# Mamba block: output weights centred once, variance of the output tiles summed on ScalarE

## The chip, the cores and the metric

The kernel runs on one core of a Trainium2 chip. The metric is the device time of one execution in microseconds (us). One core has five engines that run side by side, each with its own instruction queue worked off in order: TensorE (PE; its weight loads are listed apart as PEld), VectorE (DVE), ScalarE (ACT), GpSimd (POOL) and SyncE (SP, which here only issues DMAs).

## The reference, cut to what matters

The program is a network of several layers on an image of 2 x 256 channels x 32 x 32. The first layer after a group normalisation is a pair of Mamba blocks, and only this layer is touched. The sequence is the image itself, 1024 tokens of 256 channels, two of them in the batch.

```python
def layernorm(x, w, b):
    mu = jnp.mean(x, axis=-1, keepdims=True)
    var = jnp.mean(jnp.square(x - mu), axis=-1, keepdims=True)
    return (x - mu) * jax.lax.rsqrt(var + LN_EPS) * w + b

def mamba_block(x, ...):
    xs, res = jnp.split(u @ in_w + in_b, 2, axis=-1)   # 512 channels each
    xs = silu(conv(xs) + conv_b)                       # depthwise, 4 taps
    dt, Bm, Cm = jnp.split(xs @ xproj_w, ...)          # 16 states
    delta = softplus(dt @ dt_w + dt_b)
    dA = jnp.exp(delta * A);  dBu = delta * Bm * xs
    h = dA_t * h + dBu_t                               # scan over the 1024 tokens
    y = sum over states of h * C_t;  y = y + xs * Dp
    y = y * silu(res)
    out = y @ out_w + out_b                            # 512 -> 256 channels
    return out
...
x = x + layernorm(mamba_block(x, ...), ln1_w, ln1_b)   # likewise with m2, ln2
```

The layernorm runs over the 256 channels of `out`. Since `out` is linear in `out_w` and `out_b`, its mean over the channels is zero once each row of `out_w` (256 numbers) and `out_b` have had their own mean taken off.

## The kernel before, in words

**Units.** `layer0` (L766) cuts the 2 x 1024 tokens of each block into four chunks of 512 (`TC`), so that there are eight units, 0 to 3 for block m1 and 4 to 7 for m2. A chunk has four row tiles of 128 tokens (`TPC`), and the 512 inner channels are four chunks of 128 partitions (`NDC`).

**Steps of a unit.** `enter` (L381) makes the input projection (TensorE) and adds its bias on ScalarE (`m_pre`, L405). `front` (L408) makes the depthwise convolution as products with diagonal matrices on TensorE (L430), the projections to B, C and dt, and then `delta` and `du`: `powers` is a chain of ScalarE operations (L502, L504, L509, L511), `sums` four operations for each half, which in all units but the first GpSimd does. `scan` (L546) goes through the 16 states. For each, SyncE fetches the row of B (`m_b`), GpSimd makes h = du*b in two halves of 1024 columns, ScalarE makes exp(delta*A) into PSUM, 512 columns at a time (`m_da`, L617, three buffers), VectorE scans (L621), TensorE transposes h into PSUM tiles of tokens by channels (`m_ht`, L575 or L577, three buffers), and each tile is multiplied with C and summed: on VectorE into `m_ya` (L591), or, for the states 1, 4, 7, 10 and 13, on ScalarE into a tile of its own (`m_s`, L589), which a DMA issued by GpSimd's queue adds to `m_yb` three states later. "12_3" is the fourth channel chunk of state 12.

**The step around the change.** `back` (L641) closes a unit. It makes the gate (L655), adds up y on TensorE and multiplies with the gate on VectorE (L680 to L689), and makes the output product for the four row tiles: a row of ones times the bias row (L696) and four products with `out_sb` (L700). Two row tiles share one PSUM tile of 512 columns; the pool of these tiles has two buffers, which all the projections of all the steps share. The layernorm is `norm_rows` (L181) with ScalarE as the engine of the last step: for each row tile `bn_stats` (L188) and `bn_aggr` (L189) on VectorE, a subtraction to negate the means (L192), the logarithm and the exponential on ScalarE that give 1/sqrt(var + eps) (`rstd`, L159 and L160), a multiplication on VectorE (L200), and four scalings with scale and bias on ScalarE (L202). The normalised rows are transposed back (L213), ScalarE applies `ln_w` and `ln_b` (L724), and GpSimd adds the residual (L737). In the last unit VectorE does this with the residual in one (L717).

**What sets the order.** The scan of unit u is the frame. `paced` (L743) deals out steps of other generators to its 63 slots, one slot after each scan of 512 columns: the `front` of unit u+1, the `enter` of unit u+2, and the `back` of unit u-1, whose products and norm fall in slots 45 to 58, that is, states 11 to 14. The numbers in a part are how many steps, first slot, last slot. Each engine works its instructions off in the order that the framework's scheduler gives them; operations on GpSimd go through `net.lined` (L174, recorded as L179), which fixes their order to that of the program text. The weights of the output product come in through `load_rest` (L361, out_w at L369): for m1 before the first unit, for m2 in unit 4. The last `back` has no scan beside it: `both` (L898) mixes it with the convolution of the next layer on TensorE.

Of the kernel before, what the change touches and what calls it, by code (L numbers as in the profile page):

```python
# [10 lines left out]
F32 = mybir.dt.float32  # L11
I32 = mybir.dt.int32
BF16 = mybir.dt.bfloat16
AF = mybir.ActivationFunctionType
# [5 lines left out]
P = 128  # L20
# [4 lines left out]
C = 256  # L25
# [4 lines left out]
TPC = TC // P  # L30
DI = 512
NDC = DI // P
# [37 lines left out]
class Net:  # L70
# [83 lines left out]
        at -= self.rows_from  # L154
        return self.rows[:, at : at + w]

    def rstd(self, out, var):

        self.nc.scalar.activation(out, var, AF.Ln, bias=self.eps5)  # L159
        self.rooted = self.nc.scalar.activation(out, out, AF.Exp, scale=-0.5)  # L160

    def functions(self, which, *after):
# [18 lines left out]
    def norm_rows(self, outs, ins, by=None):  # L181


        nc, n = self.nc, len(ins)
        mv = self.small.tile([P, n, 2], F32, tag="ln_mv", name="ln_mv")
        for i, a in enumerate(ins):
            st = self.small.tile([P, 6], F32, tag="ln_st", name="ln_st")
            nc.vector.bn_stats(out=st, in_=a)  # L188
            nc.vector.bn_aggr(out=mv[:, i, :], in_=st)  # L189
        if by is nc.scalar:  # L190
            off = self.small.tile([P, n], F32, tag="ln_off", name="ln_off")
            nc.vector.tensor_sub(off, self.zeros[:, :n], mv[:, :, 0])  # L192
        rs = self.small.tile([P, n], F32, tag="ln_rs", name="ln_rs")
        if by is nc.gpsimd:
            nc.gpsimd.tensor_scalar_add(rs, mv[:, :, 1], self.eps5)
            nc.gpsimd.tensor_tensor(rs, rs, self.power[:, :n], ALU.pow)
        else:
            self.rstd(rs, mv[:, :, 1])
        if by is nc.scalar:
            nc.vector.tensor_mul(off, off, rs)  # L200
            for i, (o, a) in enumerate(zip(outs, ins)):
                nc.scalar.activation(  # L202
                    o, a, AF.Identity, scale=rs[:, i : i + 1], bias=off[:, i : i + 1]
                )
            return
        for i, (o, a) in enumerate(zip(outs, ins)):
            nc.vector.tensor_scalar(o, a, mv[:, i, 0:1], rs[:, i : i + 1], ALU.subtract, ALU.mult)

# [78 lines left out]
class Mamba:  # L287
# [73 lines left out]
    def load_rest(self):  # L361

        net, nc, m, wpool = self.net, self.net.nc, self.m, self.wpool
        in_w, out_w, xproj_w, dt_w = self.weights
        self.gate_sb = wpool.tile([P, NCC, DI], F32, tag="gate_w", name=f"{m}_gate_sb")
        nc.sync.dma_start(self.gate_sb, in_w[:, :, DI:])
        yield
        self.out_sb = wpool.tile([P, NDC, C], F32, tag="out_w", name=f"{m}_out_sb")
        nc.sync.dma_start(self.out_sb, out_w)  # L369

        if self.kept:
            nc.sync.dma_start(self.skip_tile(), self.kept[1])
        else:
            self.scaled(self.skip_tile(), f"{m}_D")
        yield

    @staticmethod
    def first(j):
# [262 lines left out]
    def back(self, j, last=False, joined=True):  # L641


        net, nc, m, xt = self.net, self.net.nc, self.m, self.xt
        y, *sums = self.chunks.pop(j)
        tok = slice(j * TC, (j + 1) * TC)
        gate = self.one.tile([P, NDC, TC], F32, tag="gate", name=f"{m}_gate_{j}")
        for dc in range(NDC):
            ps = self.ps_mm.tile([P, TC], F32, tag="mm", name=f"{m}_g_{j}_{dc}")
            for kc in range(NCC):  # L650
                nc.tensor.matmul(
                    ps, lhsT=self.gate_sb[:, kc, dc * P : (dc + 1) * P], rhs=xt[:, kc, tok],
                    start=(kc == 0), stop=(kc == NCC - 1),
                )
            nc.scalar.activation(  # L655
                gate[:, dc, :], ps, AF.Identity, bias=net.col(f"{m}_in_b", NDC + dc)
            )
            if joined and dc == NDC - 1:
                net.gates.append(gate)
            yield  # L660
        if not joined:
            with net.tc.issue_after(net.decayed.ins):
                silu = nc.scalar.activation(gate, gate, AF.Silu)
            net.functions(EXP_LN, silu)
            yield
        if last:
            tail = self.tail(f"{m}_tail_{j}")
            for cc in range(NCC):
                x = tail[:, (2 + cc) * TC : (3 + cc) * TC]
                at = j % (HW // TC) * TC  # L670
                nc.sync.dma_start(x, self.x[j // (HW // TC), cc, :, at : at + TC])
                net.lined(nc.gpsimd.tensor_scalar_add, x, x, net.col(f"{m}_ln_b", cc))
                net.lined(nc.gpsimd.tensor_add, xt[:, cc, tok], xt[:, cc, tok], x)
                yield

        if not last:
            sums = sums[:1]
        for dc in range(NDC):
            ps = self.ps_mm.tile([P, TC], F32, tag="mm", name=f"{m}_y_{j}_{dc}")
            nc.tensor.matmul(  # L680
                ps, lhsT=self.skip[:, dc, :], rhs=y[:, dc, :], start=True, stop=False
            )
            for k, ya in enumerate(sums):
                for i in range(TPC):
                    nc.tensor.matmul(
                        ps[:, i * P : (i + 1) * P], lhsT=ya[:, i, dc * P : (dc + 1) * P],
                        rhs=net.ident, start=False, stop=(k == len(sums) - 1 and i == TPC - 1),
                    )
            nc.vector.tensor_mul(y[:, dc, :], ps, gate[:, dc, :])  # L689
            yield  # L690
        found = []
        for i in range(TPC):
            if i % 2 == 0:
                ps = self.ps_mm.tile([P, TC], F32, tag="mm", name=f"{m}_out_{j}_{i}")
            a = ps[:, i % 2 * C : (i % 2 + 1) * C]
            nc.tensor.matmul(  # L696
                a, lhsT=net.ones_row, rhs=self.out_b, start=True, stop=False
            )
            for dc in range(NDC):
                nc.tensor.matmul(  # L700
                    a, lhsT=y[:, dc, i * P : (i + 1) * P], rhs=self.out_sb[:, dc, :],
                    start=False, stop=(dc == NDC - 1),
                )
                if dc == 1:
                    yield
            found.append(a)
            yield
        if not last:
            tail = y.rearrange("p d t -> p (d t)")
        inputs = []  # L710
        tiles = [tail[:, i * C : (i + 1) * C] for i in range(TPC)]
        net.norm_rows(tiles, found, nc.scalar)
        yield
        for cc in range(NCC):
            ps = net.transposed(self.ps_mm, tiles, cc, "mm")
            if last:
                nc.vector.scalar_tensor_tensor(  # L717
                    xt[:, cc, tok], ps, net.col(f"{m}_ln_w", cc), xt[:, cc, tok],
                    ALU.mult, ALU.add,
                )  # L720
                yield
                continue
            r = tail[:, (2 + cc) * TC : (3 + cc) * TC]
            nc.scalar.activation(  # L724
                r, ps, AF.Identity, scale=net.col(f"{m}_ln_w", cc), bias=net.col(f"{m}_ln_b", cc)
            )
            if self.x is not None:
                x = self.one.tile([P, TC], F32, tag="x", name=f"{m}_x_{j}_{cc}", bufs=2)
                at = j % (HW // TC) * TC
                nc.sync.dma_start(x, self.x[j // (HW // TC), cc, :, at : at + TC])  # L730
                inputs.append(x)
            yield
        if last:
            return
        for cc in range(NCC):
            r = tail[:, (2 + cc) * TC : (3 + cc) * TC]
            net.lined(nc.gpsimd.tensor_add, xt[:, cc, tok], xt[:, cc, tok], r)  # L737
            if self.x is not None:
                net.lined(nc.gpsimd.tensor_add, xt[:, cc, tok], xt[:, cc, tok], inputs[cc])
            yield  # L740
# [25 lines left out]
def layer0(net, x, x_dram, m1, m2, load_image, taps, conv_dram, lg):  # L766
# [4 lines left out]
    tc, nc = net.tc, net.nc  # L771
    with (
# [45 lines left out]
        for u, (m, j) in enumerate(units):  # L818
# [4 lines left out]
            steps = [(b, NDC, 4, 20) for b in done]  # L823
# [19 lines left out]
                steps.append((blocks[1].fetch_diagonals(), 1, 34, 35))  # L843
            rest = m.load_rest() if u and j == 0 else iter(())
            steps += [(rest, 1, 37, 38)]
            for n, first, end in Mamba.STEPS:
                steps += [(f, n, first, end) for f in fronts]
            steps += [(b, 8, 45, 53) for b in done]
# [1459 lines left out]
```

## Time and profile before

| | |
|---|---|
| median of three runs | 2036.39 us (2035.79 to 2037.86) |
| the profiled execution's own time | 2038.11 us |
| its span in the trace | 2036.4 us |
| granted TensorE clock, mean | 0.968 |
| TensorE busy | 1864.1 us (92%), 9938 products |
| VectorE busy | 1333.6 us (65%), 2141 instructions |
| GpSimd busy | 1070.5 us (53%), 726 |
| ScalarE busy | 946.7 us (46%), 1713 |

By stage, busy us in stretches of about one unit (the last two rows are the end of the Mamba layer and all the rest):

| stretch | length | PE | DVE | ACT | POOL |
|---|---|---|---|---|---|
| 15 to 120 (opening, unit 0) | 105 | 89.76 | 83.20 | 71.76 | 80.73 |
| 120 to 237 (unit 1) | 117 | 97.80 | 107.78 | 89.53 | 98.49 |
| 237 to 354 (unit 2) | 117 | 102.88 | 107.10 | 91.71 | 100.29 |
| 354 to 472 (unit 3) | 118 | 105.84 | 107.97 | 90.83 | 100.63 |
| 1000 to 1042 (last `back`) | 42 | 41.12 | 18.14 | 4.52 | 9.66 |
| 1042 to 2036 (other layers) | 994 | 939.05 | 440.99 | 222.11 | 239.37 |

How to read the lines of the profile further down. A row of a group names line, engine, operation, result<-operands with partitions x elements, and the count; after the first bar the busy time in us and the mean of one in ns; after the second the engine's idle time just before these instructions and what ended most of it ("<-POOL m_h L179": the wait for GpSimd's m_h ended last). A row of a timeline begins with the start in us and the duration; brackets show the idle time just before and what ended it. In a window's row stand the stretch, its length and, for each engine, the busy us and the number of instructions. A row of DMA issues ends with KB each and us from issue to landing.

### The profile page before, as it was taken

The page shows a single profiled execution, that of the slowest core. Times are in us where ns is not written, and L with a number is a line of the kernel's source. Part 1 is how long each engine was busy: PE and PEld are TensorE (multiplying, and loading weights), DVE is VectorE, ACT ScalarE, POOL GpSimd, SP SyncE. Part 2 cuts the span into 40 slices and gives each one's busy share as a digit, 9 for nine tenths or more (in the row PEclk, how much of TensorE's full clock was granted, in tenths as well). Part 3 has the DMA queues.
Part 4 walks back from the last instruction along what each step waited for, and adds up shares of the span by engine and source line. Part 5 has one row for each costly group of instructions (what it writes and reads, how often), then busy time and mean ns, then how long its engine had stood idle before and what let it go on. Part 6 is the DMA issues. An engine that isn't in the chain of part 4 may idle for free. (4 is left out here: it accounts for less than half of the span.)

```text
span 2036.4 us, 27880 instructions
## 1 busy us (share of the span) xinstructions
PE 1864.1 (92%) x9938; PEld 1339.2 (66%) x9938; DVE 1333.6 (65%) x2141; ACT 946.7 (46%) x1713; POOL 1070.5 (53%) x726
## 2 busy tenths in 40 slices
PE   8788988988898988899999999999999899999995
PEld 3464665656565665655656555668999666799994
DVE  6988998998889989898515285774222345652223
ACT  4777777777887767764302253332111123221111
POOL 7888796978979698985405250012333100033330
PEclk8989999999999999899999999999999999999997
DMA  4334354343435334361130100147999300359995
GB/s 151 98 91 118 86 126 133 83 118 82 131 98 140 81 86 112 87 158 47 31 57 1 52 1 1 42 179 265 322 334 343 140 21 21 143 206 319 328 329 182
DMA packets 98856, 271.77 MB, mean 133 GB/s; under 512 B 35915, under 2 KB 54224, under 8 KB 82324
## 3 DMA queue, kind: packets, MB, share of 16 engines
q1 hardware_dynamic: 81268, 198.03, 29.0%
q0 software_dynamic: 14432, 68.31, 13.5%
q10 hardware_dynamic: 3008, 3.55, 0.5%
q8 instruction: 83, 1.36, 0.3%
q14 instruction: 65, 0.53, 0.1%
HBM read 200.80 MB, written 22.77 MB: 110 GB/s over the span
## 5 line engine op out<-in xcount | busy, mean ns | idle before, releaser
L179 POOL TENSOR_TENSOR m_h<-m_du,m_b 128x1024 f32<-128x1024 f32 x254 | 604.5, 2473 | 140.7 <-PE m_ht L577 59.0
L617 ACT ACTIVATE m_da<-m_delta,m_aneg 128x512 f32<-128x512 f32 x512 | 349.4, 694 | 149.6 <-DVE m_h L621 144.5
L621 DVE TENSOR_TENSOR_SCAN m_h<-m_da,m_state,m_h 128x512 f32<-128x512 f32 x256 | 313.9, 1266 | 22.5 <-POOL m_h L179 14.7
L577 PEld LDWEIGHTS m_ht<-ident,m_h 128*128 128x128 f32 x1600 | 194.0, 146 | 193.5 <-issue 65.6
L621 DVE TENSOR_TENSOR_SCAN m_h<-m_da,m_h 128x512 f32<-128x512 f32 x256 | 298.9, 1204 | 19.3 <-ACT m_da L617 13.4
L577 PE MATMUL m_ht<-ident,m_h 128*128 128x128 f32 x1600 | 255.1, 287 | 60.2 <-DVE m_h L621 28.8
L591 DVE SCALAR_TENSOR_TENSOR m_ya<-m_ht,m_ct,m_ya 128x512 f32<-128x512 f32 x324 | 231.3, 732 | 54.8 <-PE m_ht L577 49.8
L2067 PEld LDWEIGHTS h<-xts,we_l_late 128*128 128x128 f32 x2048 | 239.6, 193 | 9.0 <-issue 4.2
L2067 PE MATMUL h<-xts,we_l_late 128*128 128x128 f32 x2048 | 241.0, 276 | 4.5 <-SPq L2129 1.7
L2075 DVE TENSOR_TENSOR hid<-hid,h 128x512 f32<-128x512 f32 x79 | 54.2, 686 | 235.1 <-PE h L2067 234.7
L1806 POOL DMA_INDIRECT x_l_early<-l_zs,l_source x15 | 17.3, 1154 | 341.1 <-ACT pt L1570 138.9
L2074 ACT ACTIVATE hid<-h 128x512 f32<-128x512 f32 x79 | 47.1, 597 | 315.0 <-PE h L2067 315.0
L575 PE MATMUL m_ht<-ident,m_h 128*128 128x128 f32 x896 | 136.8, 300 | 30.1 <-ACT m_s L589 13.2
L575 PEld LDWEIGHTS m_ht<-ident,m_h 128*128 128x128 f32 x896 | 120.5, 206 | 53.2 <-DVE m_h L621 17.1
L1806 POOL DMA_INDIRECT x_l_late<-l_zd,source x64 | 65.4, 1022 | 148.0 <-PE xt L2050 143.9
L2082 PE MATMUL o<-we_l_late,hid 128*128 128x256 f32 x512 | 122.7, 381 | 4.1 <-DVE y L2087 2.8
L2089 POOL DMA_INDIRECT l_yd<-y,target x64 | 65.4, 1022 | 106.8 <-DVE y L2087 94.5
L589 ACT ACTIVATE m_s<-m_ht,m_ct 128x512 f32<-128x512 f32 x156 | 104.4, 686 | 29.8 <-DMA m_yb<-m_s 14.8
L430 PE MATMUL m_conv<-m_pre,m_taps 128*128 128x512 f32 x240 | 115.8, 600 | 2.5 <-ACT m_xs L436 2.5
L2082 PEld LDWEIGHTS o<-we_l_late,hid 128*128 128x128 f32 x512 | 91.8, 190 | 15.3 <-DVE y L2087 3.9
L1001 PE MATMUL early_acc<-x,early 128*98 128x448 f32 (+24 forms) x308 | 98.6, 446 | 0.4 <-DVE lg L1018 0.4
L1001 PE MATMUL acc<-x,pair 128*98 128x416 f32 (+21 forms) x308 | 93.4, 451 | 0.0
(412 smaller groups left out, 3117.4 us busy)
## 6 DMA issues: line engine op xcount, KB each, us to landing
we_l_late<-in_l_experts_dram SPq DMA_DIRECT2D x64, 1536.0 KB, 9.1
m_yb<-m_s POOLq DMA_DIRECT2D x39, 1024.0 KB, 8.6
m_b<-m_bd SPq DMA_DIRECT2D x128, 256.0 KB, 3.5
we_l_early<-in_l_experts_dram SPq DMA_DIRECT2D x15, 1536.0 KB, 8.9
m_ya<-m_yb POOLq DMA_DIRECT2D x7, 1024.0 KB, 8.9
w<-in_l_w_dram SPq DMA_DIRECT2D x21, 256.0 KB, 6.2
l_yl<-l_yd SPq DMA_DIRECT2D x8, 512.0 KB, 11.9
l_zd<-l_z SPq DMA_DIRECT2D x7, 512.0 KB, 3.2
```

The lines of the kernel that those rows point to most:

```text
L179: self.line = do(*args, **named)
L430: nc.tensor.matmul(ps, lhsT=self.taps[:, dc * 4 + k, :], rhs=pre[:, dc, k : k + TC], start=(k == 0), stop=(k == 3),)
L575: nc.tensor.matmul(a, lhsT=h, rhs=net.ident, start=True, stop=True)
L577: nc.tensor.transpose(a, h, net.ident)
L589: nc.scalar.activation(to[:, i, :], ps, AF.Copy, scale=c)
L591: nc.vector.scalar_tensor_tensor(ya[:, i, :], ps, c, ya[:, i, :], ALU.mult, ALU.add)
L617: net.decayed = nc.scalar.activation(da, delta[:, dc, :], AF.Exp, scale=self.aneg[:, i : i + 1])
L621: nc.vector.tensor_tensor_scan(h, da, h, 0.0 if first else state[:, n, dc : dc + 1], ALU.mult, ALU.add)
L1001: nc.tensor.matmul(a[:, lo - 16 * k : hi - 16 * k, co : co + n], lhsT=lhsT, rhs=self.x[:, kc, b, lo - r0 : hi - r0, ci : ci + n], start=(u ...
L1806: nc.gpsimd.indirect_dma_start(out=x, out_offset=None, in_=rows[:, :], in_offset=bass.IndirectOffsetOnAxis(ap=source[:, g : g + 1], axis=0 ...
L2067: nc.tensor.matmul(ps[:, at], lhsT=w12[:, s, kc, at], rhs=xt[:, kc * P : (kc + 1) * P], start=(kc == 0), stop=(kc == NCC - 1),)
L2082: gate.o = nc.tensor.matmul(ps[:, :C], lhsT=ht[:, mc * P : (mc + 1) * P], rhs=w[:, 8 + mc, :], start=(mc == 0), stop=(mc == NHC - 1),)
```

## The change

Each block gets a step `centre`, run on ScalarE once: for each of the four chunks of `out_w` and for the bias row, a copy in place that also sums each row (`accum_out`), two scalings of the sums by -1/256, and five additions in place of these negative means. It is a part of ten steps with the slots 6 to 36 of the block's second unit (units 1 and 5), that is, ahead of the block's first output product in slot 45 of the same unit. With centred weights the output tiles have no mean, and `back` norms them without `norm_rows`: after the product of each row tile ScalarE squares the tile and sums the squares (the squares themselves go to a tile that nobody reads), `rstd` takes the sums with a scale of 1/256, and four ScalarE copies scale the tiles. `bn_stats`, `bn_aggr`, the negation and the multiplication on VectorE go, eight times each (the first two 32 times). `norm_rows` loses its ScalarE branch; its other callers are as before. SyncE's queue and the order of GpSimd's instructions are the same in both programs. The scheduler, which is free to move ScalarE's instructions, puts the centring of m1 and both bias rows at the head of ScalarE's queue, ahead of the first `m_pre`, and that of m2 into unit 5 at states 0 to 5.

```diff
-    def rstd(self, out, var):
+    def rstd(self, out, var, scale=1.0):
-        self.nc.scalar.activation(out, var, AF.Ln, bias=self.eps5)
+        self.nc.scalar.activation(out, var, AF.Ln, bias=self.eps5, scale=scale)
         self.rooted = self.nc.scalar.activation(out, out, AF.Exp, scale=-0.5)
...
             nc.vector.bn_stats(out=st, in_=a)
             nc.vector.bn_aggr(out=mv[:, i, :], in_=st)
-        if by is nc.scalar:
-            off = self.small.tile([P, n], F32, tag="ln_off", name="ln_off")
-            nc.vector.tensor_sub(off, self.zeros[:, :n], mv[:, :, 0])
         rs = self.small.tile([P, n], F32, tag="ln_rs", name="ln_rs")
...
-        if by is nc.scalar:
-            nc.vector.tensor_mul(off, off, rs)
-            for i, (o, a) in enumerate(zip(outs, ins)):
-                nc.scalar.activation(
-                    o, a, AF.Identity, scale=rs[:, i : i + 1], bias=off[:, i : i + 1]
-                )
-            return
...
+    def centre(self):
+        nc, w = self.net.nc, self.out_sb
+        sums = self.wpool.tile([P, NDC + 1], F32, tag="centre", name=f"{self.m}_centre", bufs=1)
+        parts = [(w[:, dc, :], sums[:, dc : dc + 1]) for dc in range(NDC)]
+        parts.append((self.out_b, sums[:1, NDC:]))
+        for a, s in parts:
+            nc.scalar.activation(a, a, AF.Copy, accum_out=s)
+            yield
+        nc.scalar.activation(sums[:, :NDC], sums[:, :NDC], AF.Copy, scale=-1.0 / C)
+        nc.scalar.activation(sums[:1, NDC:], sums[:1, NDC:], AF.Copy, scale=-1.0 / C)
+        for a, s in parts:
+            nc.scalar.activation(a, a, AF.Identity, bias=s)
+            yield
...
-        found = []
+        found, squares = [], net.small.tile([P, TPC], F32, tag="ln_sq", name="ln_sq")
+        square = self.one.tile([P, C], F32, tag="square", name=f"{m}_square_{j}")
         for i in range(TPC):
...
+            nc.scalar.activation(square, a, AF.Square, accum_out=squares[:, i : i + 1])
             found.append(a)
             yield
...
-        net.norm_rows(tiles, found, nc.scalar)
+        rs = net.small.tile([P, TPC], F32, tag="ln_rs", name="ln_rs")
+        net.rstd(rs, squares, 1.0 / C)
+        for i, (o, a) in enumerate(zip(tiles, found)):
+            nc.scalar.activation(o, a, AF.Copy, scale=rs[:, i : i + 1])
         yield
...
+            if j == 1:
+                steps.append((m.centre(), 10, 6, 36))
```

The second half of a PSUM tile (row tiles 1 and 3) now has a product that waits for ScalarE's square of the first half, by the dependence that the framework keeps for each tile.

## The prediction

> **What bounds the kernel now.** I read the page's engine lines first, then busy time by stage, the groups of instructions of the Mamba stage, and last the timelines of single engines around one norm. All eight norms that the change touches lie in the first 1042 of the 2036.4 us.
>
> ```profile
> core 0: us, PE busy (x) PEld busy (x) DVE busy (x) ACT busy (x) POOL busy (x), PEclk, DMA share, GB/s
> ...
> 260.00:385.00 125.00, 109.12 (x584) 75.27 (x583) 115.22 (x133) 97.64 (x177) 107.77 (x53) 0.97 0.45 119
> ...
> 880.00:1000.00 120.00, 118.02 (x514) 70.34 (x513) 91.69 (x103) 62.26 (x91) 69.64 (x36) 1.00 0.31 78
> ```
>
> One unit (512 tokens of one block) takes 116 to 119 us. Up to about 880 us VectorE is the busiest engine (115.22 of 125), but GpSimd has 107.77 and TensorE 109.12. In the last unit TensorE is the bound (118.02 of 120). Averages do not say who is waited for, so I go on to the rows that leave and to those that stay.
>
> ```profile
> L188 DVE BATCH_NORM_STATS2 ln_st<-m_out 128x6 f32<-128x256 f32 x32 | 12.3, 417 | 14.7 <-PE m_out L700 14.2
> ...
> L200 DVE TENSOR_TENSOR ln_off<-ln_off,ln_rs 128x4 f32<-128x4 f32 x8 | 7.1, 884 | 4.4 <-ACT ln_rs L160 4.3
> ...
> L189 DVE BATCH_NORM_AGGREGATE ln_mv<-ln_st 128x2 f32<-128x6 f32 x32 | 5.0, 162 | 0.0
> ...
> L192 DVE TENSOR_TENSOR ln_off<-zeros,ln_mv 128x4 f32<-128x4 f32 x8 | 2.6, 326 | 0.0
> ```
>
> VectorE loses 12.3 + 7.1 + 5.0 + 2.6 = 27.0 us of 1333.6, or 3.4 us a norm. Now the time in which the first of them stands (254 to 272 us), on GpSimd and VectorE:
>
> ```profile
> 237.41 2.37 POOL L179 TENSOR_TENSOR m_du<-m_e,m_du 128x1024 f32<-128x1024 f32 x1 [3.01 <-ACT m_du L511]
> ...
> 303.93 2.35 POOL L179 TENSOR_TENSOR m_h<-m_du,m_b 128x1024 f32<-128x1024 f32 x1 [0.24 <-PE m_ht L577]
> ```
> ```profile
> 296.29 1.22 DVE L621 TENSOR_TENSOR_SCAN m_h<-m_da,m_h 128x512 f32<-128x512 f32 x1 [0.41 <-POOL m_h L179]
> ```
> ```profile
> 237.00:304.00 67.00, 66.04 (x33) 0.97 0.40 101
> ```
>
> The first two are neighbours in the list of GpSimd's idle times: between them it never idles, and the window says 66.04 busy of 67.00. In that stretch it makes du and delta of the next unit (eight operations of 2.36 us) beside the h of the states. The same stretch comes again at 354.85, 473.83, 589.42 and 707.49, 71 to 75 us long. I paired each h with the scan that reads it. The lead of GpSimd is about 10 us at states 7 to 10, 1 to 6 us at states 12 to 15, where the norm sits, and at state 3 of the next unit it is 0.0, 0.0, 0.0, 0.6, 0.0 and 0.1 us for units 2 to 7. So in each unit VectorE catches up with GpSimd some 25 us behind the norm.
>
> **What the change costs and saves.**
>
> VectorE, six norms ahead of 880 us: 6 x 3.4 = 20.3 us of work leave. For the time to follow, the scan of state 3 would have to start earlier. It starts at 296.29 because its h ends at 296.26 on a GpSimd that has been busy since 237.41 and whose order the change leaves as it was. What is late next is that h; the freed time turns into waiting. Credit: the sum of the six leads, at most 0.7 us; I take 0. If GpSimd had slack, it would be the 20.3.
>
> Does GpSimd gain? The GPSIMD Engine Reference of the Trainium skill, section "Specifications", says that GpSimd shares its SBUF interfaces with VectorE, in contention with VectorE instructions that have two SBUF inputs; L192 and L200 are such.
>
> ```profile
> 269.35 1.73 DVE L200 TENSOR_TENSOR ln_off<-ln_off,ln_rs 128x4 f32<-128x4 f32 x1 [0.51 <-ACT ln_rs L160]
> ```
>
> This multiplication of four columns ends at 271.08, and GpSimd's operation of 268.72 ends at 271.07 after 2.35 us, as long as its neighbours. If contention cost both sides, GpSimd would win up to 0.9 + 0.3 us a norm, 7 us over six, and as GpSimd is the bound they would count. By the row VectorE alone pays: 0. I take the row.
>
> ScalarE, per norm: four squares come. No row shows one. The nearest are below.
>
> ```profile
> L1100 ACT COPY xk<-xk 128x256 f32<-128x256 f32 x16 | 6.0, 372 | 50.1 <-PE xk L1096 50.1
> ...
> L1558 ACT ACTIVATION_READ_ACCUMULATOR pr<-sc,mx 128x1 f32 x16 | 3.1, 197 | 0.0
> ```
>
> A sum costs its own instruction of 0.197. The square itself lies between 0.37 (copy from PSUM) and 0.56 (L202, two pointers): 0.57 to 0.76 with the read. I take 0.6, as it has no pointer. The four scalings lose their bias, of 0.56 us at most 0.1 each. Net 4 x 0.6 - 0.4 = 2.0 us a norm, 16 in all. The skill's page ScalarE: Activation LUTs, "Rules for kernel authors", tells one to use VectorE for multiplications and additions. By rows the pair L188 + L189 is 0.58 on VectorE and the square 0.6 on ScalarE, so as work the move is even; by that rule it loses. What decides is the queue.
>
> In ScalarE's new order the squares stand among the exponentials m_da of states 12 and 13, and ScalarE there runs without a gap from 248.98 to 258. Shifting each row by 0.6 per square, m_da 12_2 ends at 253.25, where its scan started at 252.98; the scans of 12 and 13 stay within 0.3 us of where they were, as VectorE has no statistics left to do. L511, which GpSimd takes up at 261.41, moves from 256.75 to about 258.2: still covered. Behind that:
>
> ```profile
> 266.43 1.26 ACT L589 ACTIVATE m_s<-m_ht,m_ct 128x512 f32<-128x512 f32 x2 [2.58 <-DMA m_yb<-m_s]
> ```
>
> m_s 13_0 waits for a DMA that GpSimd issued at 256.17. It stood behind m_da 14_2; now it and an L724 stand ahead of it, so m_da 14_2 ends at 266.43 + 0.69 + 0.77 + 0.69 = 268.6 and its scan moves from 267.6 to 268.6. Without L200 in VectorE's queue scan 14_3 is level again (270.65 for 271.01), and scan 0_0 of the next unit about level too (279.3 for 279.54), with one L591 (0.7 us) more behind it. Cost per norm: 0 to 1.0 us; from six I take +1.0 in all, nearer to nothing, because state 3 waits for GpSimd anyway.
>
> TensorE gets a new wait: the square of row tile 0 (and 2) reads a PSUM tile whose other half is the next product's, and that product now waits for ScalarE. Queued behind it are the transposes m_ht, and for those wait L591, m_s and the h buffers. In the new order four to nine transposes lie between (over 1 us); the square needs 0.6 and ends by about 256.5, when TensorE still waits for scan 12_3. Cost 0; bare, 2 x 0.7 us a norm.
>
> Centring. Of m1 it stands at the head of ScalarE's queue, ahead of the first m_pre, and waits for the weights' load.
>
> ```profile
> m_out_sb<-in_m_out_w_dram SPq DMA_DIRECT2D x1, 512.0 KB, 7.2
> ```
> ```profile
> 15.34 0.69 ACT L405 ACTIVATE m_pre<-m_in,cols_sb 128x512 f32<-128x512 f32 x1 [4.28 <-PE m_in L399]
> ```
>
> The load is issued at 6.29 and lands at 13.5. Four sums of about 0.5 us follow: 15.55. Queued behind is m_pre 0, ready at 15.34; +0.2. The rest is dealt out between the other three, which end up to +0.8 late. Their convolutions on TensorE keep it busy back to back, so its last product at 28.37 moves by 0.1 to 0.5 us. I take +0.4; if the bias row lands later than the weights, up to +2. Of m2 ten instructions (about 5 us) go into unit 5; three us of them into states 0 and 1, against 2.6 us of ScalarE's idle time there (1.14, 0.48, 1.02): +0.4, up to +1.5.
>
> Unit 7 is TensorE's: 0. Last norm, nothing beside it: bn_stats at 1036.5 to the last scaling at 1040.3 is 3.75 us; now a square 0.6, L159 0.3, L160 0.2, four scalings about 1.8 and the waits between: some 3.1. That is -0.6.
>
> Sum: 0 + 1.0 + 0.4 + 0.4 - 0.6 = +1.2 us.
>
> **The rivals.**
>
> Faster, VectorE is the bound: 91% busy speaks for it, the leads of 0.0 at state 3 against. Then -20.3 + 0.4 + 0.4 - 0.6 = -20 us: 2016. A part of it can come by order alone: in units 2 to 6 two L591 (1.46 us) now stand ahead of state 5's scan, in time in which VectorE may wait; kept in all five, and with the leads and a tail of -1, it is -9: 2027.4.
>
> Slower, ScalarE's queue: m_da 14_2 behind m_s 13_0 and its DMA. Price 1.0 us at each of six norms, and it decides once this lateness is still there at state 3, where GpSimd's lead is 0. With the opening at +2 and m2 at +1.5: +9.5, or 2046.
>
> That squares cost no engine time anywhere (the change does nothing) gives 2036.4 and can't be told from mine.
>
> **How the numbers follow.** The profiled execution took 2038.11 us with its span of 2036.4; the median of the three runs is 2036.39, 1.7 lower, and the differences are put on the median: 2036.4 + 1.2 = 2037.6. A measurement can tell 0.2%, 4.1 us. Absorbed, within that: 0.45. Slower by the queue: 0.33. Faster by more: 0.22, of which full relief 0.08. Range 2027 to 2046, from the partial gain to the price of the queue; outside, 0.08 below and 0.12 above.
>
> **What would show it.** Right: GpSimd's stretch from L511 to state 5 still 66 to 75 us; VectorE about 27 us less busy and idle more, waiting for m_h at states 0 to 3 and for m_da at 14; ScalarE about 28 us busier. Wrong: the waits for m_h gone, or a GpSimd operation under 2.3 us (contention paid back); TensorE waiting for ScalarE's squares; a first scan over 1 us later.

## The result and the profile after

The changed kernel takes 2060.39 us (median of four runs, 2058.59 to 2063.53) against 2037.12 us for the kernel before (four runs): 23.3 us more, ratio 1.0103 with a 95% interval of 1.0081 to 1.0124. The prediction said 2037.6 with a range of 2027 to 2046, so the time lies outside the range and on the slow side of it. The profiled execution took 2059.88 us with a span of 2058.2, 21.8 over the span before. From the last scan of the Mamba layer on, both kernels take the same time (1032.6 us before, 1033.3 after), and in the stretch up to it the granted TensorE clock is 0.95 in both; the loss lies in the Mamba layer, and the clock does not explain it.

First the page's engine lines of the changed kernel, then its busy time in the two stretches shown for the kernel before.

```profile
PE 1874.8 (91%) x9938; PEld 1343.6 (65%) x9938; DVE 1313.3 (64%) x2061; ACT 964.5 (47%) x1811; POOL 1070.5 (52%) x726
```
```profile
core 0: us, PE busy (x) PEld busy (x) DVE busy (x) ACT busy (x) POOL busy (x), PEclk, DMA share, GB/s
260.00:385.00 125.00, 108.07 (x570) 72.52 (x570) 107.77 (x113) 97.22 (x184) 105.19 (x52) 0.97 0.44 115
880.00:1000.00 120.00, 115.01 (x521) 69.69 (x520) 100.55 (x104) 65.39 (x105) 81.94 (x42) 1.00 0.48 108
```

VectorE lost 20.3 us of work and ScalarE gained 17.8; GpSimd's 726 instructions take the same 1070.5 us, yet in the first stretch every engine is less busy than before. There the time is lost in waiting, not in work. The new operations on ScalarE cost what was expected of them (mean in ns after the bar's comma):

```profile
L712 ACT ACTIVATE m_square<-m_out 128x256 f32<-128x256 f32 x32 | 12.2, 381 | 46.9 <-PE m_out L706 46.9
...
L722 ACT ACTIVATE m_xs<-m_out,ln_rs 128x256 f32<-128x256 f32 x28 | 10.9, 469 | 0.0
...
L712 ACT ACTIVATION_READ_ACCUMULATOR m_square<-m_out 128x1 f32 x32 | 6.4, 201 | 0.0
```

Where the time goes is seen from the scans, which are the frame of a unit. I subtracted the start of each state's first scan before from that after. At state 0 of units 2 to 7 the changed kernel stands at -3.6, +0.4, +4.6, +9.2, +16.5 and +22.1 us; at the last state of the last unit at +21.1. The growth lies between state 0 and state 3: 5.2, 3.7, 4.1, 8.9 and 3.4 us in units 2 to 6, together 25.3. At the states of the norm, 12 to 14, nearly nothing is lost. Single executions differ by one or two us (the first scan alone lies up to 2 us apart in runs with the same opening), so only the sum is to be trusted. What ScalarE waits for between 120 and 900 us, the two longest entries after, and the entry of the same kind before (in all, times, longest):

```profile
ACT m_da L622 <- DVE m_h L626: 97.9, 146, 3.5
ACT m_xs L441 <- POOL x L179: 29.5, 5, 7.9
```
```profile
ACT m_xs L436 <- POOL x L179: 8.9, 5, 4.2
```

One instruction in each of the units 2 to 6 waits 20.6 us longer in sum. It is the copy of the first convolution product of the next unit from PSUM, the memory that TensorE writes (L436 before, L441 after), and it waits for GpSimd's second residual addition. The two share nothing but a tile: the copy writes a new `m_xs`, whose buffer is one of three, and the last reader of that buffer is the residual addition, which reads the normed rows that `back` laid into it in the unit before. Here is ScalarE's timeline at that place in unit 2, after and before.

```profile
280.73 0.69 ACT L622 ACTIVATE m_da<-m_delta,m_aneg 128x512 f32<-128x512 f32 x1 [0.97 <-DVE m_h L626]
286.14 0.69 ACT L441 ACTIVATE m_xs<-m_conv,cols_sb 128x512 f32<-128x512 f32 x1 [4.72 <-POOL x L179]
286.72 0.18 ACT L569 COPY m_state<-m_h 128x2 f32<-128x2 f32 x1
286.81 0.69 ACT L622 ACTIVATE m_da<-m_delta,m_aneg 128x512 f32<-128x512 f32 x1
```
```profile
287.19 0.69 ACT L617 ACTIVATE m_da<-m_delta,m_aneg 128x512 f32<-128x512 f32 x1 [0.33 <-DVE m_h L621]
288.46 0.69 ACT L436 ACTIVATE m_xs<-m_conv,cols_sb 128x512 f32<-128x512 f32 x1 [0.57 <-POOL x L179]
```

After, the exponential in front of the copy is m_da 1_1 and those of 1_2 and 1_3 are queued behind it; before, it was 1_3. The program's text is the same at this place. The scheduler put the copy two exponentials earlier in units 2 and 3, three in unit 4 and two in units 5 and 6 (behind 1_0 where it was behind 1_2). VectorE runs out of exponentials (the first two lines are unit 2 after; then its waits between 120 and 900 us for m_da, before and after, and for GpSimd's m_h, before and after):

```profile
287.60 1.22 DVE L626 TENSOR_TENSOR_SCAN m_h<-m_da,m_h 128x512 f32<-128x512 f32 x1 [1.59 <-ACT m_da L622]
289.87 2.48 DVE L626 TENSOR_TENSOR_SCAN m_h<-m_da,m_h 128x512 f32<-128x512 f32 x2 [1.05 <-ACT m_da L622]
```
```profile
DVE m_h L621 <- ACT m_da L617: 12.7, 21, 1.4
DVE m_h L626 <- ACT m_da L622: 49.5, 54, 3.0
DVE m_h L621 <- POOL m_h L179: 9.5, 13, 2.0
DVE m_h L626 <- POOL m_h L179: 5.6, 7, 1.2
```

The copy's wait cannot end sooner, because GpSimd, in whose fixed order the addition stands between the h of the states, has no idle time there (window over states 0 to 2 of unit 2, after: the stretch, its length, then PE, PEld, DVE, ACT and POOL):

```profile
275.90:293.50 17.60, 11.90 (x50) 6.33 (x49) 14.88 (x15) 8.57 (x16) 17.60 (x11) 0.90 0.66 162
```

VectorE's idle time by state, summed over units 2 to 6, agrees: at states 1 and 2 it is 3.0 + 2.5 us before and 15.4 + 9.7 after.

### The profile page after: what moved, and what is told of

Same layout as the page of the kernel before. It is cut to its first block, busy times and chain, and to the rows that moved or that the text cites. A ratio compares the mean times of both kernels' runs of the same rounds, so it can differ in the third digit from the quotient of the medians.

```text
span 2058.2 us, 27947 instructions
## 1 busy us (share of the span) xinstructions
PE 1874.8 (91%) x9938; PEld 1343.6 (65%) x9938; DVE 1313.3 (64%) x2061; ACT 964.5 (47%) x1811; POOL 1070.5 (52%) x726
## 5 line engine op out<-in xcount | busy, mean ns | idle before, releaser
L435 PE MATMUL m_conv<-m_pre,m_taps 128*128 128x512 f32 x240 | 121.5, 619 | 8.5 <-ACT m_xs L441 8.4
```

The costliest lines, as they stand in the source:

```text
L435: nc.tensor.matmul(ps, lhsT=self.taps[:, dc * 4 + k, :], rhs=pre[:, dc, k : k + TC], start=(k == 0), stop=(k == 3),)
```

## The experiments

Theory A: the loss is the place of this copy in ScalarE's queue. Rival B: it is the squares, by their work or their order near the norm. Rival C: it is the centring. "Last scan" is the start of the last scan of the Mamba layer in the profiled execution: 1003.8 before, 1024.9 after. Ratios are to the kernel before, run on the same chip, with 95% intervals.

**Centring alone (e1).** The kernel before, with `centre` and its step added and `norm_rows` left as it was.

```diff
+            if j == 1:
+                steps.append((m.centre(), 10, 6, 36))
```

> The kernel before plus the centring alone; the norm with bn_stats stays as before (on centred tiles it gives the same rows). In this build the first copy of a unit's convolution (m_xs<-m_conv) keeps its place behind m_da 1_3 in ScalarE's queue in units 2, 3 and 4, behind 1_2 in unit 6, and moves to behind 1_1 in unit 5 only. Theory A (the loss is the wait of that copy at GpSimd's residual add, since the squares' build puts it two or three exponentials earlier in ScalarE's queue): only unit 5 loses, 1 to 4 us; 2035 to 2041. Rival B (the loss is the squares' own work and order on ScalarE at states 12 to 14): 2036 to 2038. Rival C (the centring costs the 23 us): 2055 to 2061.

Measured: 0.9996 (0.9985 to 1.0007). Centring costs nothing that can be measured, and rival C falls.

**Squares without centring (e2).**

```diff
-            if j == 1:
-                steps.append((m.centre(), 10, 6, 36))
```

> The changed kernel without the centring: the weights and bias keep their means, so the norm divides by the root mean square and takes no mean off. The copy stands where it stands in the changed kernel (behind m_da 1_1 or 1_0). Theory A: still slow, the wait of the copy at GpSimd's add 25 to 30 us over five units against 8.9 before; 2053 to 2060. Rival B: the same, 2053 to 2060, but without a growth of that wait. Rival C: back to 2035 to 2039.

Measured: 1.0115 (1.0096 to 1.0134), last scan at 1019.4, and the copy waits 29.9 us over five units for GpSimd. That fits A and, but for the wait, B as well. Of the 25.2 us by which its span is longer than before, 15.6 have arisen by the last scan; the other 9.6 lie in the later layers, which get other data in this kernel.

**The copy put back (e3).** The changed kernel in full; only the copy of the first product is held behind an exponential. Its step is dealt out from slot 3 instead of 0, so that this is m_da 1_3 in every unit.

```diff
+            with ExitStack() as order:
+                if dc == 0 and not alone:
+                    order.enter_context(net.tc.issue_after(net.decayed.ins))
                 silus.append(nc.scalar.activation(
...
-            steps += [(f, Mamba.HEAD - 3, 0 if u else 10, 25) for f in fronts]
+            steps += [(f, Mamba.HEAD - 3, 3 if u else 10, 25) for f in fronts]
```

> The changed kernel complete, with the one copy held behind the latest exponential in the program text and its step dealt out from slot 3 instead of slot 0, so that it stands behind m_da 1_3 in ScalarE's queue in every unit. Squares, scalings and centring as in the changed kernel. Theory A: the wait of the copy falls to at most 9 us and the time with it: 2060 - 20 = 2040, down to 2028 if VectorE's freed 3.4 us a unit now count. Rivals B and C: 2058 to 2062, nothing moves.

Measured: 0.9972 (0.9960 to 0.9984), last scan at 996.9. The whole loss is gone with all squares, scalings and the centring in place, and 0.28% beyond it. The copy's own wait is 0.4 us in all, as the profile of this kernel has it, and in unit 2 it goes through at once:

```profile
284.18 0.69 ACT L625 ACTIVATE m_da<-m_delta,m_aneg 128x512 f32<-128x512 f32 x1 [0.33 <-DVE m_h L629]
284.81 1.25 ACT L597 ACTIVATE m_ya<-m_ht,m_ct 128x512 f32<-128x512 f32 x2
286.07 0.69 ACT L444 ACTIVATE m_xs<-m_conv,cols_sb 128x512 f32<-128x512 f32 x1
```

It starts at 286.07 where it started at 286.14 in the changed kernel. It is no earlier; what stood behind it is.

**The copy early in the kernel before (e4).** Nothing of the change, but m_da 1_1 is held behind the copy.

```diff
+            if dc == 0:
+                net.entered = silus[-1]
...
-                with net.tc.issue_after(net.loaded.ins):
+                ahead = net.entered if (n, dc) == (1, 1) else net.loaded
+                with net.tc.issue_after(net.loaded.ins), net.tc.issue_after(ahead.ins):
```

> The kernel before with one thing changed: m_da 1_1 is held behind the copy of the first convolution, so that the copy stands behind m_da 1_0 in every unit, as in units 4 to 6 of the changed kernel. Statistics on VectorE, no squares, no centring. Theory A: the wait of the copy grows from 8.9 to some 30 us over five units and the time by 15 to 25: 2051 to 2062. Rivals B and C: 2035 to 2039.

Measured: 1.0065 (1.0046 to 1.0084), 13 us, last scan at 1016.7. The place alone makes the kernel before slower, by some two thirds of what A expected at the middle. The wait that A named grew much less than expected, to 12.3 us and not to 30:

```profile
ACT m_xs L436 <- POOL x L179: 9.1, 4, 3.3
ACT m_xs L436 <- PE m_ht L579: 3.2, 1, 3.2
```

The second line is unit 6. The trace puts that wait down to TensorE, but the copy starts at 769.18, 0.03 us after the addition has ended, as it does in the other units. VectorE shows the loss (unit 3 of this kernel):

```profile
409.44 4.91 DVE L624 TENSOR_TENSOR_SCAN m_h<-m_da,m_state,m_h 128x512 f32<-128x512 f32 x4 [2.90 <-ACT m_da L620]
```

The wait is shorter than in the changed kernel because ScalarE gets to the copy later, about 7 us behind the unit's first scan; in the changed kernel it gets there after 3.7 to 5.7 us. The addition ends 8 to 12 us behind that scan in both. So the place alone does not make up the 23 us: the changed kernel also reaches the place sooner, and waits 29.5 us there.

The price of a wait depends on the place. Before, it fell at a moment when VectorE still had two scans to do; behind m_da 1_0, the same wait has no such cover, and 12.3 us of waiting cost 13.

**What the copy waits for, moved (e5, e6).** The two residual additions go from GpSimd to VectorE; e5 has e3's pin, e6 has none, so that its copy stands exactly where the changed kernel's does.

```diff
-            net.lined(nc.gpsimd.tensor_add, xt[:, cc, tok], xt[:, cc, tok], r)
+            nc.vector.tensor_add(xt[:, cc, tok], xt[:, cc, tok], r)
```

> The changed kernel with the copy pinned behind m_da 1_3 (as in e3), and the two residual additions of the tail (x<-x,m_xs, 128x512, 1.25 us each on GpSimd) made by VectorE. Theory D (with the copy out of the way GpSimd is the bound, its lead at state 3 being 0.0 to 1.1 us): GpSimd has 2.5 us a unit less in units 2 to 6, so 5 x 2.5 = 12.5 us less than e3: about 2021. Rival (VectorE or ScalarE is the bound once the copy is pinned): 2032 to 2040, VectorE having 1.4 us a unit more.

> The changed kernel, the copy not pinned: in ScalarE's queue it stands behind m_da 1_1 or 1_0, exactly where it costs 23 us. Only the residual additions go to VectorE, so that what the copy waits for is no longer queued behind the h operations on GpSimd. Theory A: the loss is gone although the place is the same, as e5 within 6 us: 2016 to 2030. Rival A' (the place costs by itself, by TensorE's products or the exponentials put back): 2040 to 2060.

Measured: e5 0.9992 (0.9975 to 1.0008), e6 0.9995 (0.9977 to 1.0013). e6 settles A against A': in the place that costs 23 us, the copy waits for GpSimd in no unit once the addition is early, and e6 is as fast as e5. In unit 2 the copy follows its exponential at once:

```profile
282.11 0.69 ACT L622 ACTIVATE m_da<-m_delta,m_aneg 128x512 f32<-128x512 f32 x1 [0.97 <-DVE m_h L626]
282.73 0.67 ACT L441 ACTIVATE m_xs<-m_conv,cols_sb 128x512 f32<-128x512 f32 x1
```

e5 missed: I expected 12.5 us from a GpSimd that is relieved of 2.5 us a unit, and it is no faster than e3, if not slower. A likely part of the reason is what the additions cost on VectorE:

```profile
L750 DVE TENSOR_TENSOR x<-x,m_xs x14: 662/1638/2629, 265.3 to 1002.2; 128x512 f32<-128x512 f32 x14
```

The columns are the shortest, median and longest duration in ns: 14 like operations between 0.66 and 2.63 us. GpSimd pays too. In each of the 12 additions beside it, the GpSimd operation that comes next takes 2.68 to 2.82 us; beside the additions of e12 below, whose second operand is not in SBUF, it takes 2.38 or less. Here is one of each, e5 and then e12:

```profile
270.11 2.79 POOL L179 TENSOR_TENSOR m_delta<-m_delta,m_e 128x1024 f32<-128x1024 f32 x1
```
```profile
271.82 2.37 POOL L179 TENSOR_TENSOR m_delta<-m_delta,m_e 128x1024 f32<-128x1024 f32 x1
```

The 14 additions, at 1.25 us each, should have freed 17.5 us of GpSimd; against e3 its busy time falls by 11.1 (1070.3 to 1059.2), and VectorE's rises by 17.8 (1312.6 to 1330.4).

**VectorE's relief without squares (e7, e8).** Is it the squares that make the scheduler move the copy, or the work that left VectorE? In e7 the statistics are taken out of the kernel before and a constant is put in their place; e8 is e7 with e3's pin.

```diff
+            if by is nc.scalar:
+                nc.vector.tensor_copy(mv[:, i, :], self.zeros[:, :2])
+                continue
             st = self.small.tile([P, 6], F32, tag="ln_st", name="ln_st")
             nc.vector.bn_stats(out=st, in_=a)
```

> The kernel before without bn_stats and bn_aggr: mean and variance of the output tiles are constants (a copy of two zeros per row tile, 32 small VectorE copies), so nothing is normed by the tiles' own statistics; no squares, no centring. In this build, too, the copy stands behind m_da 1_1 or 1_0. Theory E (it is VectorE's relief, not the squares, by which the scheduler puts the copy early, and that costs the time): slow, wait of the copy 25 to 30 us, 2048 to 2058. Rival B (squares on ScalarE): as fast as before or faster, 2017 to 2037.

> As e7, with the copy pinned behind m_da 1_3. What VectorE's relief alone is worth at best. Theory D (GpSimd bound): 2028 to 2036, within 4 us of e3, which then also says that the squares cost next to nothing. If VectorE were the bound: 20 us under the kernel before, 2017. If the squares of e3 cost as much as 1 us a norm: 6 to 8 us under e3, 2026 to 2028.

Measured: e7 1.0185 (1.0152 to 1.0218), e8 1.0230 (1.0205 to 1.0254). The copy of e7 waits 28.2 us, as theory E (that VectorE's relief is what moves it) expected, but the times of both lie above what any theory expected. The profile of e8 says why (VectorE, then GpSimd, in unit 2):

```profile
292.38 12.58 DVE L203 TENSOR_TENSOR ln_off<-ln_off,ln_rs 128x4 f32<-128x4 f32 x1
304.89 4.55 DVE L627 TENSOR_TENSOR_SCAN m_h<-m_da,m_h 128x512 f32<-128x512 f32 x4
```
```profile
295.17 9.77 POOL L179 TENSOR_TENSOR m_h<-m_du,m_b 128x1024 f32<-128x1024 f32 x4
308.92 0.59 POOL L179 DMA_DIRECT2D m_yb<-m_s  x1 [3.98 <-ACT m_s L595]
```

The multiplication of four columns that was left in, no longer waiting for any statistics, was scheduled among states 1 and 2, where GpSimd runs without a pause, and took 12.58 us: until GpSimd's row of four h operations was over at 304.94. Four such multiplications make 50 us; in e7 four of them make 26 (4.7 to 10.4 us each). So the times of these two kernels say nothing of VectorE's relief.

**The relief in a fair form (e10, e11).** The kernel before, with nothing of the norm left on VectorE. e10 has e3's pin; e11 is e10 without it.

```diff
+        if by is nc.scalar:
+            nc.scalar.activation(rs, ins[-1][:, :n], AF.Ln, bias=self.one, scale=0.0)
+            self.rooted = nc.scalar.activation(rs, rs, AF.Exp, scale=-0.5)
+            for i, (o, a) in enumerate(zip(outs, ins)):
+                nc.scalar.activation(
+                    o, a, AF.Identity, scale=rs[:, i : i + 1], bias=self.zeros[:, :1]
+                )
+            return
```

> A fair form of e8: the kernel before with nothing of the norm on VectorE (no bn_stats, bn_aggr, and neither of the two small operations ln_off, one of which waited 12 us for GpSimd in e8), the logarithm and exponential on ScalarE kept on a constant, scalings kept with a bias of zero; the tiles are passed on without a norm. No squares, no centring; the copy pinned behind m_da 1_3. Theory D (once VectorE is relieved, GpSimd at states 0 to 3 takes over): as e3 within 3 us, ratio 0.996 to 0.999, so that squares and centring cost nearly nothing. If the squares cost 1 us a norm: 0.993. If VectorE were the bound: 0.990.

> As e10 without the pin. In this build the copy stands behind m_da 1_1 or 1_0, as in the changed kernel, although there is no square and no centring. Theory E (VectorE's relief is what makes the scheduler put the copy early, and the copy's wait is the loss): as the changed kernel within 6 us, ratio 1.008 to 1.012, the copy's wait 25 to 30 us. If the squares had a part in the loss beyond the order: under 1.006.

Measured on the whole kernel: 1.0144 (1.0121 to 1.0167) and 1.0272 (1.0250 to 1.0294), both outside what I expected. The un-normed rows change what the later layers get: in both kernels the experts work on 82 tiles of hidden values where all of the kernels above have 79. The Mamba layer is to be read alone, and the two kernels against each other, as they have the same data. The scans' groups (the last number before the shape is the start of the last scan), e10 and e11:

```profile
L633 DVE TENSOR_TENSOR_SCAN m_h<-m_da,m_state,m_h x256: 1253/1271/1284, 160.2 to 996.6; 128x512 f32<-128x512 f32 x128
```
```profile
L630 DVE TENSOR_TENSOR_SCAN m_h<-m_da,m_state,m_h x256: 1253/1270/1284, 162.6 to 1027.8; 128x512 f32<-128x512 f32 x128
```

e10 has its last scan at 996.6, e3 at 996.9, so squares and centring together cost nothing there that single executions can tell: the first scans of the two lie 1.2 us apart. e11 has its last scan at 1027.8. The copy's waits are these, e10 and e11:

```profile
ACT m_xs L448 <- POOL x L179: 2.4, 2, 1.6
ACT m_xs L445 <- POOL x L179: 27.9, 5, 7.7
```

Whole times of the two differ by 2096.16 - 2069.38 = 26.8 us, those of the changed kernel and e3 by 1.0103 - 0.9972 = 1.3%, 26.7 us. So the copy moves, and the loss comes, without a square or a centred weight: taking the norm's work off VectorE is enough. Rival B falls.

The loss follows the wait in the early place: 25.5 us more of it cost 27 here (e11 against e10), 29.1 more cost 27 in the changed kernel (against e3), and 12.3 cost 13 in e4.

**The copy late in the kernel before (e9).** e3's edit, in the kernel before. The copy comes to stand behind m_da 2_0 in units 2 to 6, one exponential later than in e3, and waits for GpSimd in none of them.

> The kernel before with the copy pinned late, behind m_da 1_3 in unit 1 and 2_0 in units 2 to 6 (in the kernel before it stands behind 1_3 or 1_2, and waits 8.9 us over five units for GpSimd's add). It tells what of e3's gain of 0.28% is the copy's place alone. If the gain is the copy's: 0.997 of before, 2030 to 2034. If it is VectorE's relief: 1.000, within 2 us.

Measured: 1.0010 (0.9997 to 1.0023). In the kernel before, the copy's wait of 8.9 us was free. The 0.28% of e3 therefore comes with the change, not with the pin; that it is VectorE's relief is inferred, as squares and centring put work in. The granted clock of the Mamba stretch is 0.97 in e3 and 0.95 in e9 and before; what part of the 0.28% that makes was not separated.

**A version meant to be faster (e12).** e3, and ScalarE writes its result back to PSUM, where VectorE's addition finds it.

```diff
-            r = tail[:, (2 + cc) * TC : (3 + cc) * TC]
             nc.scalar.activation(
-                r, ps, AF.Identity, scale=net.col(f"{m}_ln_w", cc), bias=net.col(f"{m}_ln_b", cc)
+                ps, ps, AF.Identity, scale=net.col(f"{m}_ln_w", cc), bias=net.col(f"{m}_ln_b", cc)
             )
+            nc.vector.tensor_add(xt[:, cc, tok], xt[:, cc, tok], ps)
...
-            r = tail[:, (2 + cc) * TC : (3 + cc) * TC]
-            net.lined(nc.gpsimd.tensor_add, xt[:, cc, tok], xt[:, cc, tok], r)
```

> A version meant to beat both: e3, and ScalarE writes ln_w * x + ln_b back into the PSUM tile, and VectorE adds it to the image from there instead of GpSimd from SBUF. In e5 VectorE's addition of two SBUF operands took 0.66 to 2.63 us, median 1.64, beside GpSimd; with one operand in PSUM it should take some 0.7 us as m_ya does (0.73). GpSimd loses 2.5 us a unit and VectorE gains 1.4. Theory D: 5 units x 1 to 2.5 us under e3: 2021 to 2030, ratio 0.991 to 0.995. Rival: the PSUM tile is held longer, and TensorE's projections, which share two such tiles, wait: 2034 to 2042.

Measured: 0.9963 (0.9945 to 0.9982). It beats both kernels, as e3 does, but cannot be told from e3; I had expected 4 to 13 us more. The addition itself is as cheap as hoped:

```profile
L739 DVE TENSOR_TENSOR x<-x,mm_t x14: 664/687/689, 267.5 to 992.6; 128x512 f32<-128x512 f32 x14
```

## Why the prediction was wrong, step by step

**The step that failed** is in the part on ScalarE: "Cost per norm: 0 to 1.0 us; from six I take +1.0 in all, nearer to nothing, because state 3 waits for GpSimd anyway." I followed the changed order of ScalarE's queue through the norm (states 12 to 14) and to the first scan of the next unit, found it "about level", and stopped, some five us ahead of the place where the order had changed to real harm. I took the step for a cost of work put in. What the runs showed in its place is an instruction that had been there all along, the copy, moved ahead of exponentials and waiting for GpSimd: 20.6 us longer over five units. With the copy put back (e3) the whole loss is gone. The cover was wrong too. A lead of 0.0 at state 3 means that VectorE waits there for GpSimd, so a delay is hidden only as far as it fits into that wait, and all its waits for GpSimd's h between 120 and 900 us came to 9.5 us before. The copy held ScalarE's exponentials up by 4.6 to 7.9 us in each unit, and h was then the early one: after the change, GpSimd's lead at state 3 is 3.9, 3.8, 3.8, 7.7 and 3.4 us in units 2 to 6, paired as in the prediction.

**The rival "ScalarE's queue"** named the engine and the sign. Its mechanism, m_da 14_2 behind m_s 13_0, is not the cause: states 12 to 14 lose next to nothing, and e3, which has that order, is fast. Its price was 6 us plus 3.5 for the centrings; measured are 23.

**VectorE's relief.** The rows summed to 27.0 us; the engine line fell by 20.3, as the records of neighbouring instructions overlap (busy time in the kernel before without these 80 instructions is 20.2 us less), so a norm frees 2.5 us and not 3.4. I credited 0 of it; e3, with the squares in place, shows 0.28%, or 5.7 us. The reason given, that the freed time turns into waiting, holds in kind once the copy is in place. In e3 the leads of GpSimd at state 3 are again 0.0, 0.0, 0.0, 1.1 and 0.3, and VectorE's idle time over units 2 to 6 rises from 54.6 to 67.2 us. But it rises at states 12 and 14 (6.9 to 12.2, and 3.4 to 11.6), in the places the statistics left, where the scans wait for ScalarE's m_da. And that GpSimd alone is the bound is not borne out: with 2.5 us a unit taken from it, e12 gained nothing clear over e3. GpSimd's leads at state 3 are 2.6, 2.4, 3.2, 3.8 and 0.0 us in e12, so in four of the five units its h lies ready and VectorE comes later. What holds VectorE back there was not isolated.

**GpSimd and contention.** "By the row VectorE alone pays: 0" held for these small operations: GpSimd's 726 instructions took 1070.5 us before and after. It is no rule: for the additions of e5 both sides paid.

**Squares, TensorE's new wait, centring.** A square with its read is 0.381 + 0.201 = 0.58 us (0.6 was taken), and the scalings fell from 0.563 to 0.469 us each. TensorE's next output product waited for a square three times, 0.8 us in all; five times the product for `delta` did, another 0.8 us, which the prediction had not listed. Centring was taken at +0.4 for m1 and +0.4 for m2, and e1 shows -0.04% with an interval that holds both. In the last norm the last square begins at 1057.85 and the last scaling ends at 1060.48: 2.6 us against the 3.75 of before, where 3.1 was expected.

**The signs.** VectorE does idle more, but for m_da and hardly at state 3 for m_h, whose waits fell (9.5 to 5.6 us). ScalarE is busier by 17.8 us, not 28; here too records overlap, and durations summed one by one grow by 25.4. GpSimd's unbroken stretches did not stay at 66 to 75 us: they are 61, 61, 56, 61 and 74. The first scan came 0.8 us earlier. One reading of the lines was high: by the same pairing the leads at states 7 to 10 were 5 to 9 us, not about 10; nothing rests on it.

**The range** left out 0.12 above 2046. It was built from prices near the norm; no case in it let an instruction of another step be moved.

## What to carry to other kernels

When an automatic scheduler orders the queues, a change of one engine's load can move instructions that the diff never touches (here some twenty us behind the norm); so list the instructions of each in-order queue that wait for another engine in the profile of before, and follow each of them in the new order to the end of the loop, not only around the edit. A wait costs by what is queued behind it, so its length says little until its place is known: 8.9 us were free with two scans in hand (e9), and 12.3 us with none in hand cost 13 (e4). Where a tile's buffer comes round again, its first writer waits for the last reader of the old content; holding that writer behind work that is due earlier, as e3 does, gives the time back.

## What the runs showed of the hardware

The VectorE operations with both operands in SBUF that were followed here did not get through while GpSimd was in an operation. In the kernel before, the multiplication of 128x4 (L200) took 1.73, 0.15, 1.28, 2.03, 0.29 and 1.26 us in the six norms beside GpSimd, each time ending 0.02 us after an operation of GpSimd had ended, and 0.16 us in the two norms without. In e8 it took 12.58 us, across a whole row of operations. That GpSimd had no idle time does not explain the difference, since it had next to none in the kernel before either (66.04 us busy of 67.00). What differs in the records is how far GpSimd's operations overlap. In the kernel before, the next one begins 0.04 to 0.06 us ahead of the end at which L200 comes in. In e7 and e8 the next one begins 0.27 to 0.66 us ahead of every end at which L203 does not come in, eight multiplications in all; each comes through only when the row is over. Why the operations overlap more there was not isolated.

The same addition of 128x512 took a median of 1.64 us from SBUF (e5) and 0.69 from PSUM (e12), never more than 0.69. From SBUF it ended 0.55 us after the end of a GpSimd operation, and the next GpSimd operation took some 0.44 us longer than its 2.36, so in these records the two engines took turns.

The Trainium skill's page SBUF — State Buffer, "Who interferes with whom", says that an operation with two SBUF inputs contends with a GpSimd operation that reads SBUF, that one with at most one SBUF input, outside VectorE's two-port modes, does not, and that issue order decides who blocks. The traces agree on the first two, and e5 agrees on the third. By the third, L203 in e8 should have come in after the operation that was running when it was issued; it waited through the ends of five more, so there the measurement decides.
